# Cross-attention and experts on one core: the prologue in written order, the first feed-forward group prepared inside attention

## The chip, the cores and the metric

The kernel runs on one core of one Trainium2 chip. The metric is device time in microseconds: 1758.08 us for the kernel before, the median of three runs (1758.02 to 1759.43). The profile is of one further execution.

## The reference

Sizes: 32 sequences of 100 tokens, 512 features, 16 heads of 32; all in float32.

```python
x = x + xattn(layernorm(x), ctx, ctx, WQ, WK, WV, Wfc, bfc)   # causal, so only the first 100 of 722 context rows count
h = layernorm(x)
x = x + ffn(h, gate_w, Wg, Wu, Wd, Ws_g, Ws_u, Ws_d)

# xattn: q, k, v = Q @ WQ.T, K @ WK.T, V @ WV.T; softmax(q k / sqrt(32), causal) v; then @ Wfc.T + bfc
# ffn:   scores = softmax(h @ gate_w.T); each of 16 experts takes its 12 best tokens of every sequence
#        expert: (gelu(x Wg) * (x Wu)) Wd * score, added to its tokens; a shared expert adds the same for all tokens
```

## The kernel before, in words

Every product that must be exact is made of three: each operand is split in a high part (a cast on ScalarE) and a low part (a subtraction), and `mm3` multiplies high by high, high by low and low by high. So each weight and each activation costs an ACT cast and a DVE or POOL subtraction before TensorE can use it.

**Attention** (`attention`). Keys and values are projected from the context in nine blocks of 128-row tiles, `KVB = [2, 2, 3, ...]`: `kproj(j, c)` makes one of four 128-column pieces of a block's keys, `vproj(j, i)` one 128-row tile of its values; `kkeep` and `vkeep` copy the result out of PSUM on ACT and store it to DRAM from SP's queue. A prologue loads and splits WK, WV and WQ (pieces of 256 KB, `load_wc` and `load_w`), projects blocks 0 and 1 and normalizes and turns the first four sequences (`x_load`, `x_stats`, `x_norm`, `x_turn`). Then 32 units follow, and two more that drain. Unit u handles four sequences (`sb = u // 4`) and four heads (`c = u % 4`): it projects the query (`qproj`), makes the scores and softmax of the unit before (`scores`, `sm_max` on DVE, `sm_sub` on POOL, `sm_exp` on ACT, `sm_sum` on DVE, `sm_mul` on POOL), and turns the weights of the unit before that, copies them (`p_turn` on PE, `p_keep` on ACT) and multiplies them with the values (`values`). From unit `KS` on, each unit also holds one `kproj` and, in three of four units, one `vproj` of a later block. `y_keep` stores the result to DRAM as yD.

**The order.** The units stand inside `tc.manual_schedule()`: each engine, and SP's queue of loads and stores, runs its instructions in written order. What stands outside, in before the prologue and the whole feed-forward, is placed by a planner, which may also put such instructions between those of the units on any engine, without changing the order of the units' own.

**Feed-forward** (`feed_forward`). The 25 tiles of 128 tokens are taken in groups, `GROUPS = [2, 2, 2, 2, 2, 3, 3, 3, 3, 3]`. `prep` of a group loads yD and splits it, multiplies it with Wfc, adds the bias and x (the add of the bias on POOL, line 477), normalizes, stores the normalized row for the experts, turns it (line 495) and makes the gate's logits. `ffn` then runs over eight chunks of the expert's weights (768 KB each, `load_chunk`: SP load, ACT cast, DVE subtraction): 24 products for gate and up, Gelu, 9 or 6 down products. During chunk 1 of a group the next group is prepared (`hook`). The shared expert's eight chunks are loaded once and stay. After the groups, `route` picks the tokens, and 16 experts follow.

**Memory.** Attention's pools are closed before those of the feed-forward open in the same space; a tile there waits for the last user of what lay under it. Wfc is loaded, split and, with the bias and the gate's weights, kept by the feed-forward; `K.late_dma`, the key load of unit 26 (`LATE`), holds these loads back.

Of the kernel before, what the change touches and what calls it, by code (L numbers as in the profile page):

```python
# [27 lines left out]
KS = 2  # L28
LATE = 26
BUF = dict(cr=4, raw=5, cx=8, x=6, v=2, kk=2, kt=3, vt=2, q=3, p=5, pt=5, y=2, pj=2, sc=1, tr=2)  # L30
GROUPS = [2, 2, 2, 2, 2, 3, 3, 3, 3, 3]
# [28 lines left out]
def attention(tc, K):  # L60
    nc = tc.nc
    with ExitStack() as ctx:
        def pool(name, bufs, **kw):
            return ctx.enter_context(tc.tile_pool(name=name, bufs=bufs, **kw))
# [3 lines left out]
        raw = pool("a_raw", BUF["raw"])  # L68
        crp = pool("a_cr", BUF["cr"])
        cxp = pool("a_cx", BUF["cx"])  # L70
        kkp = pool("a_kk", BUF["kk"])
        ktp = pool("a_kt", BUF["kt"])
        vtp = pool("a_vt", BUF["vt"])
        wpool = pool("a_w", 1)
        xnp.append(pool("a_xn1", 1))
        vp = pool("a_v", BUF["v"])
        qp = pool("a_q", BUF["q"])
        cst = pool("a_c", 1)
        stp = pool("a_st", 3)
        pp = pool("a_p", BUF["p"])  # L80
        ptp = pool("a_pt", BUF["pt"])
        yp = pool("a_y", BUF["y"])
        ps_kv = pool("a_kv", BUF["pj"], space=PSUM)
# [6 lines left out]
        for w in range(3):  # L90
            WH.append(wpool.tile([128, NC4, D], FR, name=f"wh{w}"))
            WL.append(wpool.tile([128, NC4, D], FR, name=f"wl{w}"))
# [3 lines left out]
        def split(hi, lo, src):  # L96
            nc.scalar.copy(hi, src)
            nc.vector.tensor_tensor(lo, src, f32(hi), ALU.subtract)

# [54 lines left out]
        def x_turn(sb, b):  # L154
            xt = cur["x", sb, b]
            tp = ps_ms.tile([128, NC4, S], F32, name="ms")
            for dk in range(NC4):
                nc.tensor.transpose(tp[:, dk, :], xt[:, dk * 128:(dk + 1) * 128],  # L158
                                    K.ident[0:S, 0:S])
            cs = slice(b * S, (b + 1) * S)  # L160
            split(cur["xh", sb][:, :, cs], cur["xl", sb][:, :, cs], tp)
# [32 lines left out]
        def kload(u):  # L194
            sb, c = divmod(u, NC4)
            kt = ktp.tile([128, SB], F32, name="kt")
            cur["dma"] = nc.sync.dma_start(kt, K.kD[:, c, sb * SB:(sb + 1) * SB])
# [66 lines left out]
        def p_turn(u, b):  # L264
            p = cur["p", u, b // 2][0]
            tp = ps_ms.tile([128, NC4, S], F32, name="ms")
            for h in range(4):
                nc.tensor.transpose(tp[0:S, h, :], p[:, b % 2, h, :], K.ident[0:S, 0:S])  # L268
            cur["tp", u, b] = tp

        def p_keep(u, b):
            pt = ptp.tile([S, 4, S], F32, name="pt")
            nc.scalar.copy(pt, cur["tp", u, b][0:S])  # L273
            cur["pt", u, b] = pt

        def values(u):
            sb, c = divmod(u, NC4)
            ys = ps_ms.tile([128, NC4, S], F32, name="ms")
            for b in range(4):
                pt, v = cur["pt", u, b], cur["v", sb, b]  # L280
                for h in range(4):
                    d0 = c * 128 + 32 * h
                    nc.tensor.matmul(ys[32 * h:32 * h + 32, b, :], v[:, d0:d0 + 32],  # L283
# [3 lines left out]
        def y_keep(u):  # L287
            sb, c = divmod(u, NC4)
            y = yp.tile([128, SB], F32, name="y")
            nc.scalar.copy(y.rearrange("p (b s) -> p b s", b=4), cur["y", u])  # L290
            nc.sync.dma_start(K.yD[c, :, sb * SB:(sb + 1) * SB], y)

        nsb = K.nsb
        NU = nsb * NC4
        nc.gpsimd.dma_start(mask, K.mask)
        load_wc(0, 0)
        for d in range(NC4):
            ctx_load(0, d)
        for d in range(NC4):
            ctx_split(0, d, nc.vector)  # L300
        for c in range(1, NC4):
            load_wc(0, c)
        for dk in range(NC4):
            load_w(1, dk)
        for c in range(NC4):
            kkeep(0, c, kproj(0, c))
        for d in range(NC4):
            ctx_load(1, d)
        for d in range(NC4):
            ctx_split(1, d, nc.vector)  # L310
        for b in range(4):
            x_load(0, b)
            x_stats(0, b)
            x_norm(0, b)
        load_wc(2, 0)
        for i in range(KVB[0]):
            vkeep(0, i, vproj(0, i))
        for b in range(4):
            x_turn(0, b)
        for c in range(NC4):  # L320
            kkeep(1, c, kproj(1, c))
        for c in range(1, NC4):
            load_wc(2, c)
        for i in range(KVB[1]):
            vkeep(1, i, vproj(1, i))
        for d in range(2):
            ctx_load(2, d)
        for d in range(2):
            ctx_split(2, d)
        for d in range(2, NC4):  # L330
            ctx_load(2, d)
        x_load(1, 0)

        NU = nsb * NC4
        blocks = range(2, len(KVB))
        with tc.manual_schedule():
            for u in range(NU + 2):
# [8 lines left out]
                jn, d = divmod(u + 2, NC4)  # L346
                jn += 2
                jl, dl = divmod(u + 4, NC4)
                jl += 2
                xs = mine and sb + 1 < nsb  # L350
                if mine:
                    kload(u)
                    if u == LATE:
                        K.late_dma = cur["dma"]
                    if jl in blocks:
                        ctx_load(jl, dl)
                    sn, bn = divmod(u + 5, NC4)
                    if sn < nsb:
                        x_load(sn, bn)
                if a is not None:  # L360
# [17 lines left out]
                if xs:  # L378
                    x_stats(sb + 1, c)
                if a is not None:  # L380
# [3 lines left out]
                if kv:  # L384
                    kkeep(j, ck, kproj(j, ck))
                if mine and c == 1:
# [6 lines left out]
                if a is not None:  # L393
                    sm_sum(a, 1)
                    sm_mul(a, 1)
                if xs:
                    x_norm(sb + 1, c)
                if mine and jn in blocks:
                    ctx_split(jn, d)
                if vv:  # L400
# [3 lines left out]
                if back is not None:  # L404
                    values(back)
            y_keep(NU - 1)


def feed_forward(tc, K):
    nc = tc.nc  # L410
    with ExitStack() as ctx:
# [331 lines left out]
```

## Time and profile before

| what | us |
|---|---|
| median of three runs | 1758.08 |
| the profiled execution's own time | 1757.8 |
| its span, first to last instruction | 1756.0 |
| PE busy (97% of the span) | 1698.6 |
| DVE, ACT, POOL busy | 854.9, 685.8, 440.8 |
| first scores | 38.4 |
| start of unit 28 | 328.5 |
| first gate product of group 0 | 397.8 |
| end of group 0 (its first result is added) | 443.3 |
| first gate product of the first expert | 917.2 |

Engines: PE is TensorE's matmul, PEld its weight load, DVE VectorE, ACT ScalarE, POOL GpSimd, SP the queue that issues nearly all loads and stores. A row of the slices gives the busy share in 40 equal parts of the span in tenths; PEclk is the granted TensorE clock. A row of a stretch begins with its bounds and its length, then busy time and number of instructions of each engine, the clock, the share of the DMA engines and GB/s. In a timeline a row is start, length, engine, line, operation, output and inputs, number, and in brackets how long the engine was idle before and what ended that.

### The profile page before, as it was taken

To read this page: it belongs to the slowest core of one execution; us is meant where nothing else is said; L and a number is where in the kernel's file an instruction comes from. 1 tells how busy PE (TensorE), PEld (TensorE's weight loads), DVE (VectorE), ACT (ScalarE), POOL (GpSimd) and SP (SyncE) were. 2 spreads that over 40 slices of the span, in tenths; PEclk is the share of its full clock that TensorE was granted. 3 is DMA by queue.
4 is the path that set the end of the run, shared out by engine and by line. 5 is a ranking of instruction groups with operands and counts; after the bars stand their busy time and mean duration, and the time that the engine had idled before them with its cause. 6 is when DMAs were issued, how large, how long until landed. Compare 5 with 4: busy or idle time off the path is not lost.

```text
span 1756.0 us, 28445 instructions
## 1 busy us (share of the span) xinstructions
PE 1698.6 (97%) x11272; PEld 1560.4 (89%) x11272; DVE 854.9 (49%) x2131; ACT 685.8 (39%) x1100; POOL 440.8 (25%) x401
## 2 busy tenths in 40 slices
PE   7999999959999999999999999999999999999996
PEld 6888888848999999999989999999999999999996
DVE  5666666665334443333454444444444445444441
ACT  4455555544222221121243444444444444444431
POOL 2777777661100110011020111110111110011111
PEclk9999999979999999999999999999999999999998
DMA  7344444364111121101053555544555554454431
GB/s 234 102 130 130 137 131 132 119 206 137 55 55 58 64 66 43 37 31 49 28 193 134 161 162 157 149 141 147 162 162 150 156 160 134 156 155 136 142 90 18
DMA packets 83652, 211.15 MB, mean 120 GB/s; under 512 B 9569, under 2 KB 36434, under 8 KB 83520
## 3 DMA queue, kind: packets, MB, share of 16 engines
q1 hardware_dynamic: 72592, 184.07, 31.8%
q0 software_dynamic: 10784, 25.21, 7.4%
q8 instruction: 88, 1.44, 0.3%
q14 instruction: 44, 0.36, 0.1%
q10 hardware_dynamic: 144, 0.07, 0.0%
HBM read 163.71 MB, written 45.60 MB: 119 GB/s over the span
## 4 chain that ended last, share of the span: by engine, by line
PE 90%; DVE 2%; DMA 2%; ACT 2%; POOL 2%; issue 1%; SPq 0%; POOLq 0%; ACTq 0%; DVEq 0%
PE gu L55 46%; PE dn L55 23%; PE kv L55 10%; PE m L55 4%; PE ms L268 2%; PE sc L227 2%; PE ms L283 1%; PE m L595 1%; POOL p L247 1%; DVE p L238 1%; PE m L495 1%; PE ms L158 1%; PE m L504 1%; DMA r<-wA 0%; ACT p L251 0%
## 5 line engine op out<-in xcount | busy, mean ns | idle before, releaser
L55 PE MATMUL gu<-xh,whl 128*128 128x384 f32 (+1 forms) x3328 | 656.8, 327 | 0.1
L55 PEld LDWEIGHTS gu<-xh,whl 128*128 128x128 f32 x3328 | 561.8, 188 | 16.8 <-ACT g L542 0.3
L436 DVE TENSOR_TENSOR whl<-wraw,whl 128x1536 fp32r<-128x1536 f32 x136 | 240.8, 1771 | 279.6 <-ACT whl L435 277.7
L55 PE MATMUL dn<-whl,hh 128*128 128x512 f32 x1168 | 362.5, 395 | 0.0
L55 PE MATMUL gu<-xl,whl 128*128 128x384 f32 (+1 forms) x1664 | 345.3, 326 | 0.0
L55 PEld LDWEIGHTS gu<-xl,whl 128*128 128x128 f32 x1664 | 285.9, 188 | 2.3
L435 ACT CAST whl<-wraw 128x1536 fp32r<-128x1536 f32 x136 | 201.0, 1479 | 136.9 <-PE dn L55 128.2
L610 POOL DMA_INDIRECT out_dram<-r,isl x48 | 77.3, 1610 | 693.7 <-ACT r L609 683.9
L546 ACT CAST hh<-g 128x384 fp32r<-128x384 f32 (+1 forms) x208 | 102.4, 492 | 380.0 <-DVE g L543 379.0
L55 PEld LDWEIGHTS dn<-whl,hh 128*128 128x128 f32 x1168 | 214.3, 188 | 33.9
L55 PE MATMUL dn<-whl,hl 128*128 128x512 f32 x584 | 225.4, 395 | 0.0
L542 ACT ACTIVATE g<-gu 128x384 f32<-128x384 f32 (+1 forms) x208 | 97.8, 470 | 270.3 <-PE gu L55 251.3
L543 DVE TENSOR_TENSOR g<-g,gu 128x384 f32<-128x384 f32 (+1 forms) x208 | 109.4, 526 | 188.6 <-PE gu L55 187.5
L547 DVE TENSOR_TENSOR hl<-g,hh 128x384 fp32r<-128x384 f32 (+1 forms) x208 | 112.4, 540 | 102.6 <-ACT hh L546 102.6
L55 PEld LDWEIGHTS dn<-whl,hl 128*128 128x128 f32 x584 | 109.5, 188 | 25.5
L247 POOL TENSOR_TENSOR p<-p,mx 100x800 f32<-100x800 f32 x64 | 97.9, 1548 | 80.2 <-DVE mx L238 76.0
L238 DVE CUSTOM_DVE_ANT_0 p<-sc,mask 100x100 f32<-100x100 f32 x512 | 95.7, 257 | 22.7 <-PE sc L227 22.7
L262 POOL TENSOR_TENSOR p<-p,sm 100x800 f32<-100x800 f32 x64 | 101.9, 1593 | 8.0 <-DVE sm L257 7.0
L488 POOL TENSOR_SCALAR rs<-mv 128x1 f32<-128x1 f32 x25 | 6.9, 278 | 341.1 <-DVE mv L486 341.1
L256 DVE TENSOR_REDUCE sm<-p 100x8 f32<-100x800 f32 x64 | 63.1, 985 | 32.2 <-ACT p L251 32.2
L590 POOL DMA_INDIRECT big<-xnD,isl x48 | 51.3, 1069 | 95.7 <-DVE isl L673 61.3
L268 PE MATMUL ms<-ident,p 100*100 100x100 f32 x512 | 57.4, 257 | 11.4 <-ACT pt L273 7.8
(116 smaller groups left out, 1659.8 us busy)
## 6 DMA issues: line engine op xcount, KB each, us to landing
wraw<-wE SPq DMA_DIRECT2D x136, 768.0 KB
xt<-x SPq DMA_DIRECT2D x32, 200.0 KB
vD<-vt SPq DMA_DIRECT2D x25, 256.0 KB
kt<-kD SPq DMA_DIRECT2D x32, 200.0 KB
v<-vD SPq DMA_DIRECT2D x8, 800.0 KB
yD<-y SPq DMA_DIRECT2D x32, 200.0 KB
r<-x SPq DMA_DIRECT2D x25, 256.0 KB
xnD<-r SPq DMA_DIRECT2D x25, 256.0 KB
```

The source lines that it names most:

```text
L55: r = nc.tensor.matmul(out, t[0][a], t[1][b], start=(first and i == 0), stop=(last and i == n - 1))
L238: nc.vector.tensor_tensor_reduce(out=p[:, bb, h, :], in0=sc[:, h, cs], in1=mask, scale=ISCALE, scalar=NEG, op0=ALU.add, op1=ALU.max, accum ...
L247: nc.gpsimd.tensor_tensor(pv, pv, mx[:, :, None].to_broadcast([S, 8, S]), ALU.subtract)
L262: nc.gpsimd.tensor_tensor(pv, pv, sm[:, :, None].to_broadcast([S, 8, S]), ALU.mult)
L268: nc.tensor.transpose(tp[0:S, h, :], p[:, b % 2, h, :], K.ident[0:S, 0:S])
L435: nc.scalar.copy(h, r)
L436: nc.vector.tensor_tensor(l, r, f32(h), ALU.subtract)
L542: nc.scalar.activation(g[:, 0:n], pg[:, 0:n], AF.Gelu)
L543: nc.vector.tensor_tensor(g[:, 0:n], g[:, 0:n], pu[:, 0:n], ALU.mult)
L546: nc.scalar.copy(hh[:, 0:n], g[:, 0:n])
L547: nc.vector.tensor_tensor(hl[:, 0:n], g[:, 0:n], f32(hh[:, 0:n]), ALU.subtract)
L610: ins = nc.gpsimd.indirect_dma_start(out=K.out, out_offset=bass.IndirectOffsetOnAxis(ap=isl[:, i:i + 1], axis=0), in_=o, in_offset=None, c ...
```

## The change

- **Prologue.** It is written as a function and stands inside the manual order, so each engine and SP's queue follow the text. K copies and stores of block 0 are written between the weight loads. The keys' loads of ctx block 2 and two splits more stand in the prologue, and V tile 1 of block 1 in unit 0. `KS` is 1 instead of 2, so K and V of the later blocks come one unit earlier and end in unit 28.
- **Pools.** What the keys and values alone need (WK, WV, raw pieces, context tiles, their copies) is on the right side of memory and closed at unit 29. The feed-forward's first pools open there.
- **Wfc, bias and gate weights.** They have memory of their own. Wfc's pieces are loaded and split in units 9 to 12 (`FC_AT`), the low part on DVE instead of POOL; bias and gate weights at the start of unit 13.
- **First group.** `GROUPS` is `[3, 2, 2, 3, 3, 3, 3, 3, 3]`. Its preparation is cut into steps (class `Prep`), written into units 29 to 32; chunk 0 of the shared expert is loaded in unit 30 and split in thirds in units 30 to 32. The other groups run the same steps as before in one piece (`run_prep`).
- **Smaller.** The PSUM tile of the transposes has 128 columns a row group instead of 100, of which 100 are used. The last y store goes to ACT's queue. The two buffers of raw chunks, and of xh and xl, are pools of one tile each, used in turn.

```diff
-KS = 2
-LATE = 26
+KS = 1
+FC_AT = 9
-GROUPS = [2, 2, 2, 2, 2, 3, 3, 3, 3, 3]
+GROUPS = [3, 2, 2, 3, 3, 3, 3, 3, 3]
...
+        def prologue():
+            nc.gpsimd.dma_start(mask, K.mask)
+            load_wc(0, 0)
+            for d in range(NC4):
+                ctx_load(0, d)
+            for d in range(NC4):
+                ctx_split(0, d, nc.vector)
+            for c in range(1, NC4):
+                load_wc(0, c)
+                if c == 1:
+                    pk = kproj(0, 0)
+                if c == 2:
+                    kkeep(0, 0, pk)
+                    pk = kproj(0, 1)
+            load_w(1, 0)
+            kkeep(0, 1, pk)
+            pk = kproj(0, 2)
+            load_w(1, 1)
+            kkeep(0, 2, pk)
+            pk = kproj(0, 3)
+            load_w(1, 2)
+            kkeep(0, 3, pk)
+            load_w(1, 3)
+            for b in range(4):
+                x_load(0, b)
+            pv = [vproj(0, 0)]
+            x_stats(0, 0)
+            x_stats(0, 1)
+            for d in range(NC4):
+                ctx_load(1, d)
+            x_norm(0, 0)
+            pv.append(vproj(0, 1))
+            x_stats(0, 2)
+            x_norm(0, 1)
+            vkeep(0, 0, pv[0])
+            x_stats(0, 3)
+            load_wc(2, 0)
+            x_norm(0, 2)
+            x_norm(0, 3)
+            vkeep(0, 1, pv[1])
+            for d in range(NC4):
+                ctx_split(1, d, nc.vector)
+            for b in range(4):
+                x_turn(0, b)
+            for c in range(1, NC4):
+                load_wc(2, c)
+            for d in range(NC4):
+                ctx_load(2, d)
+            x_load(1, 0)
+            pk = kproj(1, 0)
+            kkeep(1, 0, pk)
+            kload(0)
+            for c in range(1, NC4):
+                pk = kproj(1, c)
+                kkeep(1, c, pk)
+                ctx_split(2, c - 1)
+            ctx_load(3, 0)
+            vkeep(1, 0, vproj(1, 0))
+
         with tc.manual_schedule():
+            prologue()
             for u in range(NU + 2):
...
+                end = u - (NU - 3)
+                if end == 0:
+                    kvctx.close()
+                    F.open_first()
+                    pr = F.prep(0, ...)
+                    pr.load_y()
+                    for i in range(pr.nt):
+                        pr.load_x(i)
...
+                if FC_AT <= u < FC_AT + NC4:
+                    fr = fc_split(u - FC_AT)
+                if u == FC_AT + NC4:
+                    F.load_consts()
+                if end == 1:
+                    F.chunk0_load()
                 if a is not None:
                     scores(a)
...
+                if end == 3:
+                    pr.fc(2)
                 if a is not None:
                     sm_exp(a, 1)
                     sm_sum(a, 0)
                     sm_mul(a, 0)
                 if kv:
                     kkeep(j, ck, kproj(j, ck))
+                if end == 0:
+                    pr.split_y(0)
+                    pr.split_y(1)
+                    pr.split_y(2)
+                if end in (1, 2):
+                    pr.fc(end - 1)
+                    pr.stats(end - 1)
+                if end == 3:
+                    pr.stats(2)
...
                 if a is not None:
                     sm_sum(a, 1)
                     sm_mul(a, 1)
+                if end in (1, 2):
+                    pr.norm(end - 1)
+                    F.chunk0_split(end - 1)
+                if end == 3:
+                    pr.turn(0)
+                    pr.turn(1)
...
+                if FC_AT <= u < FC_AT + NC4:
+                    F.fc_split(u - FC_AT, fr)
+                if u == 0:
+                    vkeep(1, 1, vproj(1, 1))
...
                 if back is not None:
                     values(back)
+                if end == 3:
+                    pr.norm(2)
+                    F.chunk0_split(2)
+                    pr.turn(2)
+                    pr.logits()
             y_keep(NU - 1)
+    return pr.done()
```

The steps that the units call, as in the new file:

```python
def load_consts(self):                 # FeedForward; unit 13, written ahead of that unit's scores and softmax
    nc.sync.dma_start(self.bfc, K.bfc)
    nc.sync.dma_start(self.base, K.base)
    nc.sync.dma_start(gr, K.gwT)
    nc.gpsimd.memset(f32(gw), 0.0)
    nc.scalar.copy(gw[:, :, 0:NE], gr)
    nc.vector.tensor_tensor(gw[:, :, 32:32 + NE], gr, f32(gw[:, :, 0:NE]), ALU.subtract)

def load_x(self, i):                   # Prep
    xb = F.rp.tile([128, D], F32, name="r")
    F.nc.sync.dma_start(xb, F.K.x[self.rows(i), :])
    F.nc.gpsimd.tensor_tensor(xb, xb, F.bfc, ALU.add)

def norm(self, i):
    nc.gpsimd.tensor_scalar(rs, mv[:, 1:2], EPS, None, ALU.add)
    nc.gpsimd.tensor_tensor(rs, rs, F.K.nhalf[:, 0:1], ALU.pow)
    xn = F.rp.tile([128, D], F32, name="r")
    nc.vector.tensor_scalar(xn, self.xb[i], mv[:, 0:1], rs, ALU.subtract, ALU.mult)
    nc.sync.dma_start(F.K.xn[self.rows(i), :], xn)
```

## The prediction

> **What bounds the kernel now.** I read the page first, then busy time by stretch, then the queue of SP and the timelines around PE's holes. The page:
>
> ```profile
> span 1756.0 us, 28445 instructions
> ...
> PE   7999999959999999999999999999999999999996
> ...
> PEclk9999999979999999999999999999999999999998
> ```
>
> PE is full but for the first slice (prologue), slice 9 (end of attention, start of feed-forward) and the last, which is not touched. Stretches cut there (us; PE, PEld, DVE, ACT, POOL busy; clock; DMA):
>
> ```profile
> 0.00:38.40 38.40, 31.08 (x180) 27.17 (x180) 19.04 (x40) 18.79 (x41) 8.10 (x17) 1.00 0.77 246
> 38.40:60.70 22.30, 16.99 (x172) 15.17 (x172) 14.30 (x81) 9.31 (x18) 16.80 (x15) 0.85 0.27 74
> 328.50:397.80 69.30, 50.95 (x573) 43.55 (x570) 42.90 (x197) 33.98 (x61) 44.37 (x31) 0.83 0.56 177
> 443.30:917.20 473.90, 472.33 (x2729) 430.39 (x2728) 196.60 (x355) 106.04 (x193) 51.69 (x69) 1.00 0.18 59
> ```
>
> 38.4 is the first scores, 328.5 the start of unit 28, 397.8 the first gate product, 443.3 the end of group 0, 917.2 the first expert. PE lacks 7 + 5 us at the start and 18 us at the boundary, plus slow clock. In 443 to 917 it is full: only removed work counts there.
>
> In the prologue SP issues loads long before their data are wanted; its stores wait for ACT copies:
>
> ```profile
> 5.46 1.09 SPq L102 DMA_DIRECT2D raw<-wA  x2
> ...
> 8.71 1.18 SPq L102 DMA_DIRECT2D raw<-wA  x2
> 11.84 0.33 SPq L192 DMA_DIRECT2D kD<-kk  x1
> ```
> ```profile
> SPq L192 <- ACT kk L191: 4.8, 4, 1.9
> ```
>
> All four WV loads (L102) stand ahead of the first K store (L192). The second view is SP's waits: 4.8 us in four K stores. On ACT the splits wait for loads and the copies stand behind:
>
> ```profile
> 10.92 0.62 ACT L97 CAST wh<-raw 128x512 fp32r<-128x512 f32 x1 [2.11 <-DMA raw<-wA]
> 11.45 0.36 ACT L191 COPY kk<-kv 128x256 f32<-128x256 f32 x1
> ```
>
> Two more facts, from PE after the first scores and from POOL at the boundary:
>
> ```profile
> 47.03 0.90 PE L158 MATMUL ms<-ident,xt 100*128 100x100 f32 x4 [5.31 <-DVE xt L152]
> 47.85 1.67 PE L227 MATMUL sc<-kt,q 32*100 32x100 f32 x32
> ```
> ```profile
> 381.73 1.28 POOL L477 TENSOR_TENSOR r<-r,bfc 128x512 f32<-128x512 f32 x1 [3.22 <-DMA r<-x]
> 382.97 4.52 POOL L247 TENSOR_TENSOR p<-p,mx 100x800 f32<-100x800 f32 x2
> ```
>
> After 5.3 us idle the scores take 1.67 us instead of 0.89. And an add waiting for x holds the softmax behind it on POOL.
>
> **The Trainium skill.** "DMA: Bandwidth & Descriptors", Anatomy of one DMA: a semaphore wait is taken by the issuing sequencer before dispatch, so a waiting store holds all later loads of its queue. The trace agrees (the waits above). The same section prices a transfer at 2.0 us plus bytes over 436 GB/s: 2.6 us for a 256 KB piece, an estimate. The trace has 3.2 us from the first WK piece's issue (0.73) to its split (3.91), and 4.0 us for a lone 768 KB chunk, where the price says 3.8. "TensorE: Matmul & The Clock Gate", What's actually happening: an idle window of about 3.4 us halves the clock. The trace agrees: 256-wide products start every 0.21 us until 11.2 us, every 0.12 us after.
>
> **Prologue: +14.6.** In the built program's order SP now reads: WK0, context x4, WK1, WK2, K store, WK3, WV0, K store, WV1, K store, WV2, K store, WV3, x x4, context 1 x4, V store, WQ0, V store, WQ1 to 3. On ACT each K copy stands behind the split of the WV piece before it. So each WV load waits for the previous one to land, be split, a copy, and a store. WK2 lands about 7, its split ends 8.2, K copy 8.6, store, WK3 issued 9.1, WV0 9.7; both split by 13.2, K copy 13.5, store, WV1 at 14.0. A link is landing 2.5 (chosen just under the price, since no other load is in flight; the trace has no lone 256 KB load to settle it) + split 0.62 + copy 0.37 + store issue 0.35 + semaphores 0.15 = 4.0: WV2 at 18, WV3 at 22, split by 25.6 where before it was 15.6. The first V product ends about 26.5, the second, on a cold clock, 31.5 (before 21.0). WQ0 waits for the first V store (28.1), lands 31.2; the second norm pair on DVE stands behind its split, then the context splits, so turns 2 and 3 of x end at 36.7. From there PE owes K of block 1 (two cold at 2.6, two at 1.4), two V at 2.8, Q at 2.4, one turn: 16.3. Scores at 53.0, before 38.36. Bounds: links of 3.0 give +11, of 4.6 +17. The "last products moved into the first units" are one V product, still ahead of the first scores in PE's order: nothing gained. So this part of the change does not do what it says. The first K load, which on SP waits for a K store to land (before: 25.7 to 29.2), comes at about 44 and is covered by PE's 16.3.
>
> **Units 1 to 27: +0.4.** Before: 328.49 - 38.36 = 290.1. KS = 1 puts K and V of block 2 (2.1 + 2.8) into the 5.3 us hole of unit 1: it takes 0.9 + 2.4 + 2.1 + 2.8 + 0.35 + 0.2 = 8.8. Then 20 units with V at 10.76, 6 without at 9.8 (PE waits 1.7 for a norm in each), and 3 times 1.5 for a cold clock as before: 287.3. Wfc's four splits in units 9 to 12 (ACT 0.62, DVE about 0.65 each, four issues of 0.4) lie beside the V products; uncovered, at most 2.6. The wider PSUM tiles copy the same elements (0.50 a copy): 0, or 0.1 a unit either way. Moving Wfc's subtractions off POOL frees four times 1.27 there, at the boundary, and is counted in the next item. In unit 13 the gate split is written ahead of that unit's softmax on ACT and DVE, behind six issues and 0.86 MB (at the page's peak of some 300 GB/s: landing 4.6 us into the unit). DVE's maxima, due at 1.0, and ACT's y copy, due at 0.2, wait. Followed through exp, copies and turns the unit ends 3.2 late (bounds 0 and 5): 290.5.
>
> **Unit 28 to the end of group 0: +25.6.** Before: 443.3 - 328.5 = 114.8, holding 83.4 of PE work at full clock (units, two preparations of 3.8, group 34.0), so 31.4 of idle and slow clock. After: unit 28 7.6; three units of 5.5 (scores 0.9, Q 2.4, transposes 1.4, values 0.8); the last two without Q 5.3; preparation of three tiles 11.1 (a tile: 12 products of 0.232, four transposes, its logits, 3.7); a group of three 51.0 (192 gate and up products of 0.178, 72 down of 0.232); the next preparation of two 7.6: 98.9. What stalls, times from unit 28's start:
> - The planner hoists chunk 1's load and split into units 27 and 28. Its 1.5 us cast on ACT waits for the load (3.3), holding Q and both exps: +2.5.
> - SP holds chunk 3's load until chunk 1 is split (6.9); behind it stand the y load (8.8) and three x loads (9.2 to 10.1). 2.5 MB at 300 GB/s: x lands at 15.5 to 17. POOL's three adds of 1.28 stand before unit 29's subtractions, due at 12.6: those start at 19.5. On ACT the copies of unit 27's transposed weights queue behind that exp, PE idles some 9 us and restarts cold: +12.
> - Unit 30: cold clock, 3.
> - Units 31 and 32: norms 0 and 1 stand on DVE ahead of the next unit's maxima, and wait for POOL, whose rs is written behind the last multiply: 4 to 5 us each. One costs 5, the other is in the next item.
> - Units 32 and 33: besides, ACT runs chunk 2's and chunk 4's splits (each waiting 4 us for a load issued only after the split before) ahead of unit 33's copies, and chunk 6's ahead of the first Gelu. Gate products of chunks 0 and 1, which the planner puts between, fill 8 us of this: 19 stay. The last y store, now on ACT's queue, is read only by the last group: nothing.
> Sum 41.5, so 140.4. Bounds: 22 if most loads land in time, 50 if also later chunks are late.
>
> **Group 1 on: -20.7.** 22 tiles and 20 preparations instead of 23 and 21: 17.0 + 3.7. Fewer, wider groups give nothing: by the stores of their results a group of two with its two preparations takes 41.8 us, one of three with three 61.9, 20.9 and 20.6 a tile; by the product times above 17.0 a tile remains in both when preparation is taken off.
>
> Sum: 14.6 + 0.4 + 25.6 - 20.7 = +19.9 on the profiled 1757.8 (span 1756.0, 1.8 around it): 1777.7. The median shown is 0.3 higher: 1778.
>
> **Rivals.**
> 1. Prologue bound by transfers either way: 246 GB/s over 38.4 us speaks for it, the serial chain against. Then +3 there: 1766.
> 2. Faster: the boundary pays. Wfc's 1 MB, for which ACT waited 7 us there, is gone, and gate products fill PE. Its idle must fall below 21.6 (from 41.5) to break even with my prologue; at 10 it is -12: 1746. Against it: the adds, norms and splits named above wait in order.
> 3. Later chunks also late, idle 50 and links 4.6: 1790.
>
> **How the numbers follow.** Forecast 0.60 (1768 to 1788), rival 1 0.14, rival 3 0.10, rival 2 0.12, within 0.2% (about what a measurement of this kernel can tell) 0.04. Slower 0.84. The range 1756 to 1790 leaves out rival 2 and the worst of rival 3.
>
> **What would show it.** SP: K stores between WV loads, 4 us apart, first scores near 53. Unit 13 about 14 long. POOL adds waiting for x at unit 29; ACT splits waiting for wraw before the last copies. Group 1 to first expert 453. Scores before 45, or group 0 ending within 120 of unit 28, make me wrong.

## The result, and the profile after

The changed kernel takes 1783.79 us, the median of four runs (1779.42 to 1785.3), beside 1758.76 for the kernel before (four runs, 1758.02 to 1762.09). The ratio is 1.0135, with a 95% interval of 1.0112 to 1.0158: slower by 1.35%, and the interval is far from 1. The forecast was 1778, in a range of 1756 to 1790. The profiled execution took 1785.3 us, the longest of the four, with a span of 1783.5. From its page:

```profile
span 1783.5 us, 27998 instructions
...
PE   5999999977999999999999999999999999999996
...
PEclk8999999978999999999999999999999999999999
```

The first slice of PE has fallen from 7 to 5 tenths. The boundary between attention and feed-forward now takes two slices, both at 7, where it was one at 5. The rest is as full as before. Cut at the same events as the prediction, each stage by its own trace:

| stage | before | after | difference | predicted |
|---|---|---|---|---|
| start to first scores | 38.36 | 56.32 | +18.0 | +14.6 |
| units 1 to 27 | 290.13 | 288.97 | -1.2 | +0.4 |
| unit 28 to end of group 0 | 114.8 | 143.1 | +28.3 | +25.6 |
| group 1 to first expert | 473.8 | 453.8 | -20.0 | -20.7 |
| experts and end | 838.8 | 841.3 | +2.5 | 0 |
| span | 1756.0 | 1783.5 | +27.5 | +19.9 |

**Prologue.** SP's timeline (start, length, queue and line, what is moved). L109 loads WV, L116 WK, L199 stores keys:

```profile
10.50 0.62 SPq L109 DMA_DIRECT2D raw<-wA  x1
14.79 0.33 SPq L199 DMA_DIRECT2D kD<-kk  x1
15.22 0.38 SPq L109 DMA_DIRECT2D raw<-wA  x1
19.45 0.33 SPq L199 DMA_DIRECT2D kD<-kk  x1
19.87 0.38 SPq L109 DMA_DIRECT2D raw<-wA  x1
23.91 0.33 SPq L199 DMA_DIRECT2D kD<-kk  x1
24.33 0.38 SPq L109 DMA_DIRECT2D raw<-wA  x1
```

A WV load leaves only when the K store ahead of it has left, and that store waits for a copy on ACT. SP's waits in the first 60 us say the same, in total, number of waits and longest:

```profile
SPq L199 <- ACT kk L198: 20.5, 6, 4.5
```

On ACT the copy stands behind the split of the WV piece, which waits for its load. The chain closes there:

```profile
18.53 0.62 ACT L99 CAST wh<-raw 128x512 fp32r<-128x512 f32 x1 [3.77 <-DMA raw<-wA]
19.06 0.37 ACT L198 COPY kk<-kv 128x256 f32<-128x256 f32 x1
```

From the load at 15.22 to the next at 19.87 a link is 4.65 us: 3.31 until the split starts, 0.53 until the copy, 0.39 until the store is issued, 0.42 until the next load. Three such links bring the last WV load to 24.33. With the loads of x right behind it, it takes until 28.79 to be split.

**Boundary.** POOL's timeline at unit 29:

```profile
360.94 3.70 POOL L628 TENSOR_TENSOR r<-r,bfc 128x512 f32<-128x512 f32 x3 [4.59 <-DMA r<-x]
364.60 3.00 POOL L254 TENSOR_TENSOR p<-p,mx 100x800 f32<-100x800 f32 x2
```

The three adds of the bias wait 4.59 us for x, and the softmax's subtractions stand behind them. ACT's timeline near the end of attention:

```profile
417.20 1.47 ACT L558 CAST whl<-wraw 128x1536 fp32r<-128x1536 f32 x1 [2.90 <-DMA wraw<-wE]
...
425.28 1.48 ACT L558 CAST whl<-wraw 128x1536 fp32r<-128x1536 f32 x1 [3.80 <-DMA wraw<-wE]
426.66 0.88 ACT L280 COPY pt<-ms 100x400 f32<-100x400 f32 x2
...
435.53 1.47 ACT L558 CAST whl<-wraw 128x1536 fp32r<-128x1536 f32 x1 [3.12 <-DMA wraw<-wE]
```

Casts of the shared expert's chunks 2, 4 and 6 wait 2.9, 3.8 and 3.1 us for their loads. The copies of the last turned weights (L280) and the first Gelu (at 439.25) stand behind them.

**Experts.** The last stretch was to stay as it was, and lost 2.5 us. Busy time of two experts, one after the other (bounds, length, then PE, PEld, DVE, ACT, POOL):

```profile
993.04:1044.92 51.88, 51.88 (x279) 48.55 (x278) 25.16 (x28) 23.48 (x32) 7.81 (x6) 1.00 0.50 152
1044.92:1096.54 51.62, 51.62 (x279) 48.19 (x278) 24.59 (x27) 23.01 (x31) 7.91 (x6) 1.00 0.51 152
```

PE is full in both at full clock, yet every second expert takes 0.26 us more. Before, each took 51.60.

### The profile page after: what moved, and what is told of

Same layout as the page of the kernel before. It is cut to its first block, busy times and chain, and to the rows that moved or that the text cites. A ratio compares the mean times of both kernels' runs of the same rounds, so it can differ in the third digit from the quotient of the medians.

```text
span 1783.5 us, 27998 instructions
## 1 busy us (share of the span) xinstructions
PE 1708.3 (96%) x11072; PEld 1566.8 (88%) x11072; DVE 855.8 (48%) x2120; ACT 684.4 (38%) x1086; POOL 436.2 (24%) x397
## 4 chain that ended last, share of the span: by engine, by line
PE 89%; DVE 3%; DMA 3%; POOL 2%; ACT 2%; issue 1%; SPq 0%; POOLq 0%; ACTq 0%; DVEq 0%
PE gu L55 46%; PE dn L55 23%; PE kv L55 10%; PE m L55 3%; PE ms L275 2%; PE sc L234 2%; PE ms L290 1%; DMA raw<-wA 1%; POOL p L254 1%; PE m L759 1%; DMA wraw<-wE 1%; DVE p L245 1%; PE ms L165 1%; PE m L671 1%; PE m L661 1%
## 5 line engine op out<-in xcount | busy, mean ns | idle before, releaser
L55 PEld LDWEIGHTS gu<-xh,whl 128*128 128x128 f32 x3200 | 559.6, 189 | 20.7 <-ACT g L718 4.8
L55 PEld LDWEIGHTS dn<-whl,hl 128*128 128x128 f32 x584 | 109.5, 188 | 25.6
```

The source lines that it names most:

```text
L55: r = nc.tensor.matmul(out, t[0][a], t[1][b], start=(first and i == 0), stop=(last and i == n - 1))
```

## The experiments

The theory is the prediction's: the loss is loads and copies that stand behind waiting instructions, in the prologue on SP's queue, at the boundary on POOL, DVE and ACT; the transfers themselves would fit. The main rival is that the prologue is bound by its transfers, and that stalls at the boundary are hidden behind one another. Times are medians; a ratio is against the kernel before on the same chip, with its interval, and is set against the changed kernel's 1.0135 (1.0112 to 1.0158). A stage is read from one trace, and scatters. Where the changed kernel's prologue is left as it is, first scores come at 55.6 to 57.4 us (six traces); where its boundary is, unit 28 to the end of group 0 takes 138.3 to 146.1 us (seven traces). A difference that stays within such a range shows nothing.

**1. The prologue planned again.** One line: the call moves out of the written order.

```diff
+        prologue()
         with tc.manual_schedule():
-            prologue()
```

> The changed kernel with its prologue outside the written order again, so that the planner orders it; all else stays. Theory (a serial chain of loads behind K stores costs the prologue 18 us): first scores at 38 to 42 instead of 56.3, time 1765 to 1769. Rival (the prologue is bound by its transfers either way): first scores at 52 or later, time above 1779.

The first scores come at 39.16 instead of 56.32, 17.2 earlier. The time is 1771.17, ratio 1.0060 (1.0044 to 1.0077): 0.75% or 13 us less than the changed kernel. The time is 2 us above the expected, with the kernel before at 1760.61 beside it; the stage is as expected, and the transfer rival is out: the same transfers fit in 39 us. Some 3 of the 17.2 us are lost again in this trace between unit 28 and the end of group 0, which took 146.1 us, the upper end of its scatter. SP's timeline shows what the planner does:

```profile
5.46 1.09 SPq L109 DMA_DIRECT2D raw<-wA  x2
6.59 0.75 SPq L143 DMA_DIRECT2D xt<-x  x2
9.01 1.22 SPq L109 DMA_DIRECT2D raw<-wA  x2
10.79 0.33 SPq L199 DMA_DIRECT2D kD<-kk  x1
11.17 0.80 SPq L143 DMA_DIRECT2D xt<-x  x2
```

All four WV loads and two of x have left before the first K store.

**2. WV and WK loaded ahead of the K stores, in written order.** The loads are issued first; the splits and copies keep their places.

```diff
-            load_w(1, 0)
+            rk = {c: issue_wc(0, c) for c in range(1, NC4)}
+            rv = [issue_w(1, 0), issue_w(1, 1)]
...
+            rv.append(issue_w(1, 3))
+            kkeep(0, 0, pk)
...
+            split_w(1, 0, rv[0])
             kkeep(0, 1, pk)
```

> The changed kernel, prologue still in written order, but the loads of WK and WV are all issued ahead of the first K store on SP; the order on ACT, DVE and PE is kept. Theory (the place of the stores on SP's queue alone makes the chain): WV3 split by 16, first scores at 40 to 45, time 1768 to 1773. Rival a (the written order on ACT, DVE and PE costs as much): first scores at 48 to 52. Rival b (bound by transfers): at 54 or later, time above 1780.

First scores at 46.53: 9.8 of the 17.2 come back. Time 1775.58, ratio 1.0082 (1.0059 to 1.0104). The last WV split is at 16.2, as expected, so the chain through the stores is gone. But the forecast of 40 to 45 missed: WQ's first piece still stood behind a V store (issued at 21.02, split at 25.63), and the last two norms behind that split.

**3. All loads ahead of the stores.** x, context block 1 and WQ are moved up as well (the edit is against run 2).

```diff
             rv.append(issue_w(1, 3))
+            for b in range(4):
+                x_load(0, b)
+            for d in range(NC4):
+                ctx_load(1, d)
             kkeep(0, 0, pk)
...
+            rq = [issue_wc(2, 0)]
```

> As the run with WK and WV loaded ahead of the K stores, but the loads of x, of context block 1 and of WQ also stand ahead of the stores that held them; ACT, DVE and PE keep their order. Theory (every microsecond of the prologue is a load behind a waiting store): first scores at 39 to 42, time 1766 to 1770. Rival (the written order on ACT, DVE and PE costs the rest, 7 us): first scores stay at 45 to 47.

First scores at 48.26, no earlier than in run 2, where 39 to 42 was expected: the theory as written fell. Time 1779.34, ratio 1.0105 (1.0084 to 1.0127). SP's timeline, then ACT's:

```profile
10.28 1.52 SPq L161 DMA_DIRECT2D xt<-x  x4
11.85 2.31 SPq L142 DMA_DIRECT2D cr<-ctxT  x4
14.36 0.33 SPq L217 DMA_DIRECT2D kD<-kk  x1
```
```profile
19.27 0.37 ACT L216 COPY kk<-kv 128x256 f32<-128x256 f32 x1 [7.64 <-DMA kD<-kk]
19.54 0.62 ACT L99 CAST wh<-raw 128x512 fp32r<-128x512 f32 x1
```

Keys have two buffers (kk). The first store now leaves at 14.36 and lands some 4.9 us later, among the loads; the third copy waits 7.64 us for its buffer, and WV's next split stands behind that copy on ACT. A store held back starves its buffers just as a load behind a store starves the splits.

**4. x between the first two K stores, WQ between the next two** (against run 2).

```diff
             kkeep(0, 0, pk)
+            for b in range(4):
+                x_load(0, b)
...
             kkeep(0, 1, pk)
+            rq = issue_wc(2, 0)
```

> As the run with WK and WV loaded ahead of the K stores (first scores 46.5), with the four loads of x moved up between the first and the second K store, and WQ's first piece up between the second and the third; stores keep their place before context block 1. Theory (what is left of the prologue's loss is x and WQ standing behind stores, while loading everything ahead of the stores, first scores 48.3, starved the two kk buffers instead): first scores at 40 to 43. Rival (the written order on ACT, DVE and PE): they stay at 46 or later.

First scores at 44.54, between the two readings. Time 1773.69, ratio 1.0079 (1.0063 to 1.0095), which can't be told from run 2's. ACT's timeline:

```profile
18.14 0.37 ACT L216 COPY kk<-kv 128x256 f32<-128x256 f32 x1 [3.81 <-DMA kD<-kk]
18.41 0.62 ACT L99 CAST wh<-raw 128x512 fp32r<-128x512 f32 x1
```

The fourth K copy waits for the second store to land, which four loads of x had joined, and the last WV split waits behind it. So of 17.2 us the place on SP alone gives back 11.8. For the other 5.4 the trace names ACT's written order, a split behind a copy that waits for a buffer; that order was changed only together with the rest, by the planner in run 1.

**5. The gate weights' split at the end of unit 13.**

```diff
         nc.gpsimd.memset(f32(gw), 0.0)
+
+    def consts_split(self):
+        nc, gw, gr = self.nc, self.gw, self.gr
         nc.scalar.copy(gw[:, :, 0:NE], gr)
...
                     F.fc_split(u - FC_AT, fr)
+                if u == FC_AT + NC4:
+                    F.consts_split()
```

> The changed kernel with the gate weights' split (one ACT copy, one DVE subtraction) moved from ahead of unit 13's softmax to that unit's end. Theory: unit 13 falls from 13.6 us to 10.7, as its neighbours, time 1780 to 1782. Rival (unit 13 is long for another reason, such as six issues on SP): it stays above 13 and the time at 1783.

Unit 13 takes 10.77 instead of 13.64, as the theory has it. The time does not show it: 1787.27, ratio 1.0141 (1.0116 to 1.0166). In its trace four other units take 11.9 to 12.3 instead of 10.76, where the changed kernel's has one of 13.13, and units 1 to 27 together are the same 289.0 us. What these units are is said in the last section. In the changed kernel TensorE's clock is halved in part of unit 13 as well, but runs 3, 7 and 9, with the split in its old place and full clock there, show 13.3 to 14.1 for the unit, so the split is the cause. The 2.9 us are shown for the unit and lost in the scatter for the time.

**6. The bias adds behind unit 29's last multiply.**

```diff
+                if end == 0:
+                    for i in range(pr.nt):
+                        pr.add_b(i)
...
     def load_x(self, i):
...
-        F.nc.gpsimd.tensor_tensor(xb, xb, F.bfc, ALU.add)
```

> The changed kernel with POOL's three bias adds of the first group moved from ahead of unit 29's subtractions to behind that unit's last multiply. Theory (the adds, waiting for x, hold the softmax): unit 29 falls from 16.8 us to 9 to 12, time 1776 to 1780 if nothing takes its place. Rival (what is won is given back in units 30 to 33, where norms and chunk splits wait for the same loads): unit 29 falls as much, the end of group 0 moves by less than 2, time above 1781.

Unit 29 takes 10.67 instead of 16.77, unit 30 11.92 instead of 10.09. From unit 28 to the end of group 0 it takes 136.7 us. Time 1779.32, ratio 1.0106 (1.0089 to 1.0123), about 5 us less, though the two intervals overlap: the two units are clear, the gain in time is not. POOL's timeline:

```profile
359.14 3.01 POOL L254 TENSOR_TENSOR p<-p,mx 100x800 f32<-100x800 f32 x2 [2.06 <-DVE mx L245]
...
369.41 3.78 POOL L636 TENSOR_TENSOR r<-r,bfc 128x512 f32<-128x512 f32 x3
373.16 3.00 POOL L254 TENSOR_TENSOR p<-p,mx 100x800 f32<-100x800 f32 x2
```

The subtractions no longer wait for x, and the adds no longer wait at all. They now stand for 3.8 us ahead of the next unit's subtractions, and unit 30 loses 1.8 us.

**7. rs computed right behind the statistics.**

```diff
     def stats(self, i):
...
+        nc.gpsimd.tensor_scalar(rs, mv[:, 1:2], EPS, None, ALU.add)
+        nc.gpsimd.tensor_tensor(rs, rs, F.K.nhalf[:, 0:1], ALU.pow)
...
     def norm(self, i):
...
-        nc.gpsimd.tensor_scalar(rs, mv[:, 1:2], EPS, None, ALU.add)
-        nc.gpsimd.tensor_tensor(rs, rs, F.K.nhalf[:, 0:1], ALU.pow)
```

> The changed kernel with the first group's two small POOL instructions for the norm (rs) written right behind the statistics, ahead of the last multiply; nothing else. Theory (DVE waits in the norm for rs, and the next unit's maxima behind it): unit 31 falls from 13.6 us to 10 to 11, the drain by 2 to 4 more, group 0 ends at 481 to 484 instead of 488.4. Rival (DVE's wait is hidden behind chunk splits and loads): the end of group 0 moves by less than 2.

Unit 31 takes 12.21 instead of 13.61, less of a gain than expected. From the start of unit 28 group 0 ends after 136.8 us instead of 143.1, but run 9, which alters no instruction, has 138.3 there. The time, 1781.42 with ratio 1.0120 (1.0098 to 1.0141), can't be told from the changed kernel's. Part of a gain is lost again: chunk 0's subtraction on DVE now runs beside POOL's multiply, and takes 2.02 us instead of 0.69:

```profile
386.87 2.02 DVE L571 TENSOR_TENSOR whl<-wraw,whl 128x512 fp32r<-128x512 f32 x1
```
```profile
386.67 1.67 POOL L269 TENSOR_TENSOR p<-p,sm 100x800 f32<-100x800 f32 x1 [0.29 <-DVE sm L264]
```

**8. The chunks' casts behind the last copies.**

```diff
     def p_keep(u, b):
...
-            nc.scalar.copy(pt, cur["tp", u, b][0:S, :, 0:S])
+            K.last_pk = nc.scalar.copy(pt, cur["tp", u, b][0:S, :, 0:S]).ins
...
-            self.sw[f] = self.load_chunk(0, f)
+            with self.tc.issue_after(self.K.last_pk):
+                self.sw[f] = self.load_chunk(0, f)
```

> The changed kernel with ACT's casts of the shared expert's chunks 1 to 7 queued behind the last copy of turned weights of unit 33; their loads, and all else, stay with the planner. Theory (these casts, waiting for their loads, stand ahead of the units' own work and hold the loads behind them on SP): unit 28 falls from 10.0 to 7.6, unit 29 from 16.8 to 9 to 12, the last values product starts 15 to 22 earlier, group 0 ends 10 to 18 earlier, time 1765 to 1774. Rival (what is won before is paid in group 0, whose chunks then come late): the last values come as much earlier, but group 0 ends less than 5 earlier.

Unit 28 takes 8.33 instead of 9.99. From its start group 0 ends after 131.8 us instead of 143.1, below the whole scatter, and the time is 1775.34, ratio 1.0089 (1.0073 to 1.0106): 8 us less, with intervals that do not overlap. The casts cost that much. But unit 29 stays at 16.94, against the theory. SP's timeline and POOL's:

```profile
352.14 0.32 SPq L199 DMA_DIRECT2D kD<-kk  x1
352.55 0.39 SPq L610 DMA_DIRECT2D big<-yD  x1
353.03 1.46 SPq L628 DMA_DIRECT2D r<-x  x3
```
```profile
359.21 3.70 POOL L629 TENSOR_TENSOR r<-r,bfc 128x512 f32<-128x512 f32 x3 [4.55 <-DMA r<-x]
```

No chunk load stands ahead any more, and still the loads of y and x leave only behind unit 28's K store, at 352.14. That store was what held them. The last values product starts 6.8 us earlier (422.5 instead of 429.6, from unit starts 0.2 apart), not 15 to 22. By the written order unit 33's turns of the weights stand on PE behind the third tile's norm, turn and logits.

**9. A pad of 32 bytes.** The changed kernel keeps xh and xl in two pools of one pair each. The second pair begins at 109216 and 115360, 32 bytes off a multiple of 64; the first pair, at 135936 and 142080, and both pairs of before begin at multiples of 64. The pad moves the second pair and what shares its memory: one raw buffer and the weights of chunks 1 to 7 ahead of it, the Gelu's tiles behind it.

```diff
     def open_rest(self):
...
+        pool("f_pad", 1).tile([128, 8], F32, name="pad")
         self.rawp.append(pool("f_raw1", 1))
```

> The changed kernel with a pad of 32 bytes a partition ahead of the feed-forward's second set of pools, so that the second pair of xh and xl begins at a multiple of 64 bytes, as the first does and as both did before; no instruction differs. Theory (a moving operand at an address that is a multiple of 32 but not of 64 costs the gate and up products 2 ns each): every second expert falls from 51.90 to 51.62 us, the last stretch from 841.3 to 839.0. Rival (it is the split in two pools, or the side of memory): they stay at 51.90.

```profile
985.12:1036.57 51.45, 51.45 (x280) 48.05 (x278) 25.16 (x28) 23.44 (x32) 7.80 (x6) 1.00 0.52 152
1036.57:1088.20 51.63, 51.63 (x279) 48.21 (x277) 24.59 (x27) 22.96 (x31) 7.89 (x6) 1.00 0.51 153
```

The same experts that took 51.88 us now take 51.45, less than before the change; the others stay. Group 1 on falls from 453.8 to 452.0, the last stretch from 841.3 to 837.8; in every trace of the changed kernel and its variants without the pad these two are 453.8 and 841.2 to 841.3. Time 1777.03, ratio 1.0107 (1.0083 to 1.0130), an interval that overlaps the changed kernel's. So addresses are the cause of the unforeseen 2.5 us, and the two pools as such are not, since they are still two. But the theory had the wrong operand. Counting through the groups and experts, the one that became faster multiplies the first pair, which the pad did not move; what moved of its operands are its weights.

**10. The kernel before, with its pairs moved by 32 bytes.**

```diff
+        pool("f_pad0", 1).tile([128, 8], F32, name="pad0")
         xtp = pool("f_xt", 2, reuse_waits="tile")
+        pool("f_pad1", 1).tile([128, 8], F32, name="pad1")
```

> The kernel before, with 32 bytes a partition of padding ahead of the feed-forward's four tiles xh and xl and 32 behind them, so that these begin at a multiple of 32 but not of 64 bytes, as one pair in the changed kernel does. Theory (that address costs gate and up products of 384 columns 1 to 2 ns each): every expert takes 51.85 to 51.95 us instead of 51.60, the last stretch 843 instead of 838.8, the time up by 4 to 8. Rival (the address matters only together with others of the changed kernel): experts stay at 51.60.

```profile
969.89:1021.38 51.49, 51.49 (x280) 48.13 (x278) 25.16 (x28) 23.45 (x32) 7.81 (x6) 1.00 0.51 153
```

51.49 us instead of 51.60: a little faster, where the theory said slower. Time 1757.46, ratio 0.9984 (0.9976 to 0.9993). The rule of 64 bytes has fallen. Here the pairs moved by 32 bytes and the chunks' weights by 64. What fits runs 9 and 10 is the distance between the two operands, as the last section shows.

**11. GROUPS alone, in the kernel before.**

```diff
-GROUPS = [2, 2, 2, 2, 2, 3, 3, 3, 3, 3]
+GROUPS = [3, 2, 2, 3, 3, 3, 3, 3, 3]
```

> The kernel before with one line of the change alone: GROUPS is [3, 2, 2, 3, 3, 3, 3, 3, 3] instead of [2, 2, 2, 2, 2, 3, 3, 3, 3, 3]. Theory (a tile costs 17.0 us and its preparation 3.7 in a group of two as in one of three, so the 20 us that the changed kernel saves after group 0 are only the tile moved into group 0): from unit 28 to the first expert 585 to 593 instead of 588.7, time within 4 of before. Rival (nine groups instead of ten save waits of their own): 8 or more less, time below 1752.

From unit 28 to the first expert it takes 594.0 us, one above the expected range: 141.0 to the end of group 0 and 453.0 after it. Time 1766.00, ratio 1.0033 (1.0019 to 1.0047). This one line makes nearly all of both large terms, +26.2 and -20.8, and costs 5.4 on balance. The same stretch of the changed kernel is 596.9. Busy time from unit 28 to the end of group 0, with GROUPS alone and then in the changed kernel:

```profile
328.50:469.50 141.00, 116.54 (x913) 103.13 (x910) 71.33 (x239) 55.20 (x89) 52.75 (x40) 0.89 0.42 137
```
```profile
345.30:488.40 143.10, 115.46 (x889) 102.48 (x886) 69.32 (x241) 51.92 (x86) 44.81 (x36) 0.87 0.38 120
```

PE's work, clock and idle time are alike, and 141.0 lies inside the scatter of the changed kernel's 143.1. Writing the preparation into the last units filled none of the holes on balance: the planner, with the same groups, does as well.

**12. All mended.** Runs 1, 5, 6, 7 and 9 together; casts as in run 8 for chunks 1 and 2, and for chunks 3 to 7 each behind the Gelu's cast three chunks before; and in the drain the third tile's norm, turn and logits behind the last turns and copies of weights.

```diff
                     p_keep(back, 3)
+                if end == 4:
+                    pr.norm(2)
+                    F.chunk0_split(2)
+                    pr.turn(2)
+                    pr.logits()
...
                     values(back)
-                if end == 3:
-                    pr.norm(2)
-                    F.chunk0_split(2)
-                    pr.turn(2)
-                    pr.logits()
...
+            with self.tc.issue_after(self.K.last_pk if f < 3 else self.hhs[f - 3]):
```

> The changed kernel with all mended: prologue planned, gate split and bias adds late, rs early, chunk casts 1 and 2 behind the last copies of turned weights and 3 to 7 each behind the Gelu's cast three chunks before, the pad of 32 bytes; and in the drain the third tile's norm, turn and logits behind the last turns and copies of weights instead of ahead of them. Theory (the stalls named are separate): prologue 17 less, unit 28 to end of group 0 at 113 to 123 instead of 143, feed-forward 5 less; time 1733 to 1744, below the kernel before by 0.9% or more. Rival (stalls that overlap: the first tile's statistics and softmax bound the drain anyway): unit 28 to end of group 0 stays at 128 or more, time 1748 to 1758.

```profile
span 1743.6 us, 27999 instructions
...
PE   7999999979999999999999999999999999999996
...
PEclk9999999989999999999999999999999999999998
```
```profile
328.40:453.90 125.50, 109.68 (x890) 96.43 (x887) 72.49 (x242) 51.46 (x86) 44.38 (x36) 0.90 0.43 139
```

1745.47 us, ratio 0.9916 (0.9902 to 0.9929): 0.84% faster than the kernel before, though the expected gain was missed by a little, and the stretch at the boundary lies between the two forecasts. First scores at 40.92. From unit 28 to the end of group 0 it takes 125.5 us, 17.6 less than in the changed kernel and 15.6 less than with GROUPS alone, so preparing group 0 inside attention pays once these waits are taken out. What each mend gives here was not taken apart. In the page's slices the boundary is one slice at 7 again.

## Why the prediction was right, and where its steps were off

**Prologue, +18.0 for +14.6.** The chain was right in every link: store, load, split, copy, store. The term that was off is the link, 4.65 us for 4.0, because a lone 256 KB load took 3.31 us to its split, not the 2.5 that were chosen. The 3.2 us that the trace of before shows for the first piece was the better row. The Trainium skill's "DMA: Bandwidth & Descriptors", Anatomy of one DMA, gives 2.6, an estimate that was still too low: the section states its fit for transfers that GpSimd issues, and these loads are SP's. The last WV piece was split, low part included, at 30.1 for 25.6, and 3.3 of these 4.5 us reach the first scores, at 56.3 for 53.0. "Links of 4.6 give +17" stood among the bounds. Rival 1, the transfers, is out by run 1.

**Units 1 to 27, -1.2 for +0.4.** Unit 1 took 9.13 for 8.8, unit 13 13.64 for about 14, and run 5 shows the cause to be the gate split. The rest is units with a cold clock: one besides unit 13 in this trace, for the three assumed. The 300 GB/s that the prediction calls the page's peak is not in the page, whose slices reach 234; stretches of 5 us in that trace reach 296 to 358.

**Unit 28 to the end of group 0, +28.3 for +25.6.** With the prediction's own count of PE's work, 98.9 (its terms add to 99.1), 44.2 us of idle and slow clock are left for the 41.5 predicted. The scatter of this stretch is larger than that difference, and the single terms fared worse than the sum, so that it came so near is in part luck:
- Unit 28, 2.5 for the chunk's cast: run 8 gives 1.7; without it the unit takes 8.33, not 7.6.
- Unit 29, 12: the unit took 16.8 for 17.5. The adds hold 6.1 of it (run 6). That chunk 3's load holds y and x was wrong: unit 28's K store does (run 8).
- Norm behind rs, 4 to 5 each: 1.4 in unit 31 (run 7). The drain, from the last scores to the end of group 0, is 5.6 shorter in that trace, but 4.7 in run 9's as well, so its part stays open.
- Chunk splits ahead of the copies and the Gelu: real, 8 us in time together with unit 28's (run 8). The drain took 92.7 us, where the sum had 88.2 (140.4 less 52.2 for units 28 to 31, which took 50.5); that is where it fell short. The trace has there a wait of 4.4 us on PE, for the first Gelu, which stands behind the casts of chunks 5 and 6; the sum counted only chunk 6's. That this is the whole difference is argued, not shown.

**Group 1 on, -20.0 for -20.7.** Run 11 shows this with GROUPS alone: -20.8. "Fewer, wider groups give nothing" was not quite right: the regrouping costs 5.4 us over both stages. It also puts the prediction's weights in place. Of 27.5 us in the span the prologue is 18.0 and the regrouping 5.4; the written preparation, which took most of the prediction's working, adds only 2.9, less than the scatter, and 0.8 of that is the stretch from group 1 on, where every second group multiplies the slow pair. So +25.6 was near the right number at the boundary, but not as a price of the written order: the stalls that were named are real, yet the planner leaves as much idle with the same groups.

**Experts, +2.5 for 0.** Not foreseen: the new pools brought weights to addresses at which their products with one pair are slow (run 9); that it is their distance is inferred. Rival 2, that the boundary pays, did not come. Run 12, with the waits taken out, takes 577.5 us from unit 28 to the first expert, where the kernel before takes 588.7, so it was near.

## What to carry to other kernels

On a queue that runs in written order, put a load ahead of any store that waits for a computation, but no more loads than leave the stores' buffers time to come free; the same holds for a split and a copy on one engine. Before writing out an order that a planner made, compare the two queue by queue. And when a change has several parts, run the plainest one alone: here a line of group sizes explained both large terms, which a profile of the whole change shows as two separate effects.

## What the runs showed of the hardware

**Where a product's operands lie in memory changes its speed.** A gate or up product multiplies 128 columns of weights with 384 of xh or xl. This is the mean time from one to the next in chunks 3 to 7 of an expert, by the operands' addresses in the built program, modulo 256 bytes; none of them differs in instructions or in clock:

| kernel | weights | xh, xl | weights less xh, xl | ns |
|---|---|---|---|---|
| changed, slow experts | 160 | 0 | 160 | 176.7 |
| changed, other experts | 160 | 160 | 0 | 174.5 |
| changed with pad, same as slow | 192 | 0 | 192 | 173.4 |
| changed with pad, others | 192 | 192 | 0 | 174.5 |
| before | 64 | 64 | 0 | 174.7 |
| before, shifted | 128 | 96 | 32 | 173.7 |

Neither address alone orders them: weights at 160 are in the slowest row and in a middle one, xh at 0 in the slowest and in the fastest. Equal distances give equal times. Chunk 0, whose weights lie elsewhere, gives two distances more in the same traces: 64 takes 176.6 ns (changed with pad, others), 96 takes 173.8 (changed, others). The means also hide a start. At a distance of 0 or 32 the first three to six products after another kind of product are slow, up to 185 ns, and the later ones take 173.3, as at 192; at 160 and 64 none settles there. That the distance is what counts is read from these rows; no run moved the operands and nothing else. Why 160 and 64 are bad is open.

**A wait of 1.6 us may halve TensorE's clock, or may not.** PE's timeline at the same place of two executions with the same instructions, run 9 and then the changed kernel:

```profile
136.68 0.53 PE L165 MATMUL ms<-ident,xt 100*128 100x100 f32 x4 [1.63 <-DVE xt L159]
...
137.97 1.15 PE L234 MATMUL sc<-kt,q 32*100 32x100 f32 x32
139.05 1.70 PE L55 MATMUL kv<-xnh,wh 128*128 128x400 f32 x4
```
```profile
137.51 0.53 PE L165 MATMUL ms<-ident,xt 100*128 100x100 f32 x4 [1.64 <-DVE xt L159]
...
138.79 0.96 PE L234 MATMUL sc<-kt,q 32*100 32x100 f32 x32
139.69 1.00 PE L55 MATMUL kv<-xnh,wh 128*128 128x400 f32 x4
```

The same wait is followed by products of 1.70 us in one and 1.00 in the other; the unit takes 12.25 and 10.76 us. The Trainium skill's "TensorE: Matmul & The Clock Gate", What's actually happening, says that the clock is set by an activity window that runs free of the program, so that the cold products vary from run to run. The traces agree: within each, all changes of the granted clock lie on a grid of 3.41 us (at 43.03, 138.60 and 142.01 in run 9; at 44.17, 180.70 and 184.12 in the changed kernel), and the grid lies elsewhere in each execution. In run 9 the wait falls into one window, which has 1.49 us of idle, and at its end, 138.60, the clock is halved. In the changed kernel the border at 136.33 cuts the wait into 0.46 and 1.18 us, and the clock stays. The idle window of about 3.4 us that the section names need not be idle throughout. From 40 us on, in all 14 traces, every window at full clock with more than 1.85 us of idle on PE ended in a halved clock, none with less than 1.45 did, and between these there are both.

Two to four such spells fall in units 1 to 27 of each trace. They go with the scatter of the times: run 9's kernel took 1773.82 us at a mean granted clock of 0.980 and 1783.55 at 0.975, run 5's 1779.74 at 0.979 and 1787.85 at 0.976.

**DVE slows beside POOL.** A 128x512 subtraction with two inputs took 0.69 us alone and 2.02 beside POOL's multiply (run 7), and it ended 0.55 us after that multiply. In run 5 the gate's small subtraction took 1.39 us beside two multiplies, instead of 0.22. The Trainium skill's "GPSIMD Engine Reference", Specifications, names contention with DVE instructions that read two inputs from SBUF; both traces agree.
